# Weight product of a two-layer graph network on one core: seven products over pairs of row blocks, summed in PSUM

## The chip, the core and the metric

The kernel runs on one core of a Trainium2 chip. Time is device time in microseconds (us) of one execution. A core has five engines, each working through its own list of instructions in order: PE (matrix products; it writes only to PSUM), DVE (elementwise work, transposes, maxima), ACT (activation functions and copies), POOL and SP (here mostly issuers of DMA transfers). An instruction can wait for counts that instructions of other engines raise when they end. PSUM has eight banks; one bank holds 128 x 512 float32 numbers. SBUF is the large on-chip memory.

## The reference

Two layers over 4096 nodes with 512 features, and a 4096 x 4096 matrix of zeros and ones.

```
# layer 0: mean of the first 64 neighbours, two linear maps, residual, layer norm
keep = Ab & (cumsum(Ab, axis=1) <= 64);  nb_mean = keep @ X / max(cnt, 1)
x1 = layernorm(x + leaky(x @ W_line.T + b_line) + where(cnt > 0, leaky(nb_mean @ W_nb.T + b_nb), 0))
# layer 1: attention over the neighbours, residual, layer norm
Wh = x1 @ W + bW
e  = (Wh @ a1 + b1)[:, None] + (Wh @ a2 + b2)[None, :]
e  = where(adj > 0, leaky(e, 0.2), -9e15);  attention = softmax(e, axis=1)
out = layernorm(x1 + attention @ Wh)
```

Every row of `attention` sums to one, so `attention @ (x1 @ W + bW)` equals `attention @ (x1 @ W) + bW`. The scores come from a vector computed apart (`W @ a`), not from `Wh`.

## The kernel before

**Layer 0** (to 677 us of the profile) makes x1 in 32 blocks of 128 rows and stores them to DRAM in four tensors `x1_d[0..3]`.

**The weight product**, from 677 to 787 us, is the stage that changes. It makes Wh in 32 steps `s` (loop at L1060). A step takes a block of 128 rows of x1 (a "square" in the change's words: 128 rows, whose 512 features are the contraction), turned so that the features lie on the partitions, and multiplies it with the 512 x 512 weight: four matmuls 128x512 at L1064, accumulated in one PSUM bank (`acc`). Around them:

- `load_turned` (L799 to L807, the DMAs at L804) loads square s+7 by four DMAs on SP into one of four places `x1s`; `turn_x1` (L814, transpose at L818) turns square s+3 on DVE into a tile `c` (three of them, and three early places).
- `finish_wh` (L822, at L827) adds the bias `bias_w` on DVE and writes the step's result from PSUM into `bt`. `bt` has 16 entries of 7 parts of 128x256: an entry belongs to a pair of squares s and s+4, whose four half results are parts 0 to 3. `combine_wh` (L835, L840 to L843) makes the other operands of the seven products of the attention stage from them, four subtractions on DVE.
- From s = 7 the attention weights of the first two row blocks (b = 0 and 1, four quarters i each) are made beside the products: `cover` (ACT, L863), `mask` (DVE, L873, with a maximum beside it), `score` (ACT, L856), after four quarters `greatest` (eight small DVE instructions, L886 to L893), `bend_greatest` (four small ACT instructions, L856), `less` (DVE, L910) and `weigh` (ACT exponential, L919). One quarter is masked at each step s = 8 to 15.
- At s = 22 to 28 `turn` and `combine` (L938, L951 to L954) make the operands of the first two parts of the attention product, q = 0 and 1.

**The attention stage**, from 787 us to the end, is `consume(q)` for 64 parts q (PE, L978): 28 products of matmuls 128x256 each, seven for eight over pairs of row blocks. Beside it DVE and ACT make the weights of the next blocks; the four `combine_wh` left over run in q = 0. `load_res` (L991) loads the two rows of x1 of the residual by SP, some 48 us before `end_row` (L1022) adds them; then come the layer norm and the store on POOL.

The order of each engine's work is that of the Python text: the kernel schedules by hand (`manual_schedule`), and the recording layer adds a wait wherever two engines touch the same tile; for PSUM it does so by bank.

Of the kernel before, what the change touches and what calls it, by code (L numbers as in the profile page):

```python
# [9 lines left out]
F32 = mybir.dt.float32  # L10
# [5 lines left out]
ALU = mybir.AluOpType  # L16
# [4 lines left out]
P = 128  # L21
SQ = 32
# [10 lines left out]
def two_layer_adj_gnn(  # L33
# [16 lines left out]
    nc = tc.nc  # L50
    N, C = x.shape
    NB = N // P
    NC = C // P
    NT = NB // 2
# [46 lines left out]
    def x1_blk(b):  # L101

        n, k = divmod(b // 2, 4)
        return x1_d[k].rearrange("(n q r) c -> n r q c", n=4, r=2)[n, b % 2]
# [32 lines left out]
    with ExitStack() as l0:  # L137
# [130 lines left out]
        NS = NB // KB  # L268
# [516 lines left out]
    for n in range(NC):  # L785
        nc.sync.dma_start(
            ws[ts(n, SQ), :, :], w[ts(n, P), :].rearrange("(m b) c -> b m c", b=SQ)
        )
    bias_w = ep.tile([P, C], F32, name="res", bufs=1)


    bt = big.tile([P, NS // 2, 7, HC], F32, name="bt")
# [3 lines left out]

    st_n = big.tile([P, NI, 3, NB], F32, name="st_n")

    def load_turned(s):  # L799

        if s < NS:
            part = x1_d[s // 8].rearrange("(n s a) c -> s a n c", s=8, a=SQ)[s % 8]
            for n in range(NC):
                nc.sync.dma_start(  # L804
                    x1s[ts(n, SQ), s % 4, :].rearrange("a (j c) -> a j c", c=P),
                    part[:, :, ts(n, P)],
                )  # L807

# [2 lines left out]

    FIRST = 8

    def turn_x1(s):  # L814
        if s < NS:
            t = early[:, s, :C] if s < 3 else rows.tile([P, C], F32, name="c")
            x1ts[s] = t.rearrange("p (m i) -> p m i", i=P)
            nc.vector.transpose(  # L818
                x1ts[s].rearrange("p m (j a) -> p j m a", a=SQ),
                x1s[:, s % 4, :].rearrange("p (j m b) -> p j m b", m=NC, b=SQ),  # L820
            )

    def finish_wh(s):

        kk, h = s // 8 * 4 + s % 4, s // 4 % 2
        b = bt[:, kk]
        nc.vector.tensor_tensor(  # L827
            b[:, 2 * h : 2 * h + 2, :], pws.pop(s).rearrange("p (h c) -> p h c", h=2),
            bias_w.rearrange("p (h c) -> p h c", h=2), ALU.add,
        )  # L830
        if h == 1:
            later.append(kk)

    later = []

    def combine_wh():

        if later:
            b = bt[:, later.pop(0)]
            nc.vector.tensor_tensor(b[:, 4], b[:, 1], b[:, 0], ALU.subtract)  # L840
            nc.vector.tensor_tensor(b[:, 5], b[:, 3], b[:, 4], ALU.subtract)
            nc.vector.tensor_tensor(b[:, 6], b[:, 5], b[:, 2], ALU.subtract)
            nc.vector.tensor_tensor(b[:, 1], b[:, 3], b[:, 1], ALU.subtract)  # L843

    def load_nat(b, h):

        if b < NB:
            nats[b, h] = ep.tile([P, 2, NS * SQ // 2], BF16, name="nat")
            rows = code_d[b].rearrange("(i a) (n x) -> n a i x", a=SQ, n=4)
            for n in range(4):  # L850
                nc.sync.dma_start(nats[b, h][ts(n, SQ)], rows[n][:, ts(h, 2), :])
# [6 lines left out]
    def cover(b, i):  # L858

        if i == 0:  # L860
            wts[b] = early if b == 0 else wp.tile([P, NI, NS * SQ], F32, name="w")
            m4s[b] = stat.tile([P, NI], F32, name="m4", bufs=2)
        nc.scalar.activation(  # L863
            wts[b][:, i, :], nats[b, i // 2].bitcast(U8)[:, i % 2, :],
            AF.Relu, bias=far, scale=-FAR,
        )
        if i % 2:
            load_nat(b + 1, i // 2)

    def mask(b, i):  # L870

        w_i = wts[b][:, i, :]
        nc.vector.tensor_tensor_reduce(  # L873
            w_i, e2_n, w_i, 1.0, -3e38, ALU.subtract, ALU.max, m4s[b][:, i : i + 1]
        )

    def score(b, i):
        w_i = wts[b][:, i, :]
        bend1(b, i, w_i, w_i)

    def greatest(b):
        m4 = m4s.pop(b)
        mm = stat.tile([P, NI], F32, name="mm", bufs=2)
        m2 = stat.tile([P, NI], F32, name="m2", bufs=2)
        q0, q1, q2, q3 = (slice(SQ * n, SQ * n + SQ) for n in range(4))
        nc.vector.tensor_copy(m2[q0], m4[q1])  # L886
        nc.vector.tensor_copy(m2[q2], m4[q3])
        nc.vector.tensor_tensor(m4[q0], m4[q0], m2[q0], ALU.max)
        nc.vector.tensor_tensor(m4[q2], m4[q2], m2[q2], ALU.max)
        nc.vector.tensor_copy(m2[q0], m4[q2])  # L890
        nc.vector.tensor_tensor(mm[q0], m4[q0], m2[q0], ALU.max)
        for q in (q1, q2, q3):
            nc.vector.tensor_copy(mm[q], mm[q0])  # L893
        mms[b] = mm
# [7 lines left out]
    def bend_greatest(b):  # L902
        mm = mms.pop(b)
        lms[b] = stat.tile([P, NI], F32, name="lm", bufs=2)
        for i in range(NI):
            bend1(b, i, lms[b][:, i : i + 1], mm[:, i : i + 1])

    def less(b):
        nms[b] = stat.tile([P, NI], F32, name="nm", bufs=2)
        nc.vector.scalar_tensor_tensor(  # L910
            nms[b], lms.pop(b), -1.0, st_n[:, :, 1, b], ALU.mult, ALU.subtract
        )

    def weigh(b, i):
        g, r = divmod(b, 2)
        if i == r == 0:
            z4s[g] = stat.tile([P, 2, NI], F32, name="z4", bufs=2)
        w_i = wts[b][:, i, :]
        nc.scalar.activation(  # L919
            w_i, w_i, AF.Exp, bias=nms[b][:, i : i + 1], accum_out=z4s[g][:, r, i : i + 1]  # L920
        )
        if i == NI - 1:
            del nms[b]
            if r == 1:
                nc.sync.dma_start(z_d[g], z4s.pop(g))
                zqs[g] = stat.tile([P, 2, 4], F32, name="zq", bufs=2)
                for i_ in range(NI):
                    nc.sync.dma_start(
                        zqs[g][ts(i_, SQ)],
                        z_d[g].rearrange("(n a) r i -> i a r n", a=SQ)[i_],  # L930
                    )
# [52 lines left out]
    def load_res(g):  # L984

        for b in (2 * g, 2 * g + 1):
            if b % 2:
                x1rows[b] = ep.tile([P, C], F32, name="res", bufs=1)
            else:
                x1rows[b] = rows.tile([P, C], F32, name="c")  # L990
            nc.sync.dma_start(x1rows[b], x1_blk(b))  # L991

    def end_weights(g):
        rz = stat.tile([P, 2], F32, name="rz", bufs=2)
# [37 lines left out]
    for s in range(3):  # L1032
        turn_x1(s)
        load_turned(s + 4)
    nc.sync.dma_start(bias_w, b_w.partition_broadcast(P))
    for g in range(5):
        if g == 2:
            bend0(NB - 1)
# [18 lines left out]
    for n in range(4):  # L1057
        nc.gpsimd.dma_start(st_n[ts(n, SQ)], st_d.rearrange("(i a) k b -> a i k b", a=SQ))

    for s in range(NS):  # L1060
        pws[s] = ps_acc.tile([P, C], F32, name="acc")
        x1t = x1ts.pop(s)
        for m in range(NC):
            nc.tensor.matmul(  # L1064
                pws[s], x1t[:, m, :], ws[:, m, :], start=(m == 0), stop=(m == NC - 1)
            )
        if s > 0:
            finish_wh(s - 1)
        turn_x1(s + 3)
        load_turned(s + 7)  # L1070
        if s == 0:
            load_nat(0, 0)
            load_nat(0, 1)
        k = s - FIRST
        if k in (4, 8):
            less(k // NI - 1)
        if 0 <= k < 8:
            mask(*divmod(k, NI))
        if -1 <= k < 7:
            cover(*divmod(k + 1, NI))  # L1080
        if 0 <= k < 8:
            score(*divmod(k, NI))
        if k in (3, 7):
            greatest(k // NI)
            bend_greatest(k // NI)
        if 4 <= k < 12:
            weigh(*divmod(k - 4, NI))
        if s in range(FIRST + 14, FIRST + 22, 2):
            q, part = divmod((s - FIRST - 14) // 2, 2)
            (turn, combine)[part](q)  # L1090
        elif s >= FIRST + 8:
            combine_wh()
    finish_wh(NS - 1)

    for q in range(NP * NT):
        g, k = divmod(q, NP)
        consume(q)
        more = 0 < q < NP * NT - 1
        if more:
            turn(q + 1)  # L1100

        b = {2: 2 * g + 3, 3: 2 * g + 4}.get(k, 2 if q == 0 else NB)
        if k == 3 and more:
            combine(q + 1)
        if b < NB:
            for i in range(NI):
                cover(b, i)
                mask(b, i)
            for i in range(NI):
                score(b, i)  # L1110
            greatest(b)
        if k != 3 and more:
            combine(q + 1)
        if b < NB:
            shift(b)
            for i in range(NI):
                weigh(b, i)
        while q == 0 and later:
            combine_wh()
        if k == 0 and g > 0:  # L1120
            end_weights(g - 1)
            end_low(g - 1)
            end_top(g - 1)
        if q == NP * NT - 1:
            end_weights(g)
        if k == 1:
            if g > 0:
                end_row(2 * g - 2, nc.gpsimd)
                end_row(2 * g - 1, nc.gpsimd)
            load_res(g)  # L1130
# [65 lines left out]
```

## Time and profile before

| | us |
|---|---|
| three runs | 1568.65, 1570.67, 1571.28 (median 1570.67) |
| the profiled execution's own time | 1568.37 |
| its span (first to last instruction) | 1566.6 |
| PE, DVE, ACT, POOL busy | 1557.8, 1258.2, 952.7, 238.4 |
| the weight product, 677.05 to 786.92: length | 109.87 |
| in it PE, DVE, ACT, POOL busy | 109.87, 83.43, 32.96, 7.05 |
| attention stage, 786.92 to 859.00: PE, DVE, ACT busy | 72.08 of 72.08, 60.06, 45.38 |

A row of a group reads: line, engine, operation, what it writes and reads, shapes, count, then busy time and mean ns of one, then the engine's idle time before it and what ended that. A timeline row reads: start, length, engine, line, operation, count, and in brackets the idle time before it. A float32 matmul stands as two records, of weight load (PEld) and product (PE) each. Records of PE overlap: a 128x512 record is 0.59 long, and the next begins 0.43 after it began; a 128x256 record is 0.38 long and the next begins 0.216 later.

### The profile page before, as it was taken

To read this page: it belongs to the slowest core of one execution; us is meant where nothing else is said; L and a number is where in the kernel's file an instruction comes from. 1 tells how busy PE (TensorE), PEld (TensorE's weight loads), DVE (VectorE), ACT (ScalarE), POOL (GpSimd) and SP (SyncE) were. 2 spreads that over 40 slices of the span, in tenths; PEclk is the share of its full clock that TensorE was granted. 3 is DMA by queue.
4 is the path that set the end of the run, shared out by engine and by line. 5 is a ranking of instruction groups with operands and counts; after the bars stand their busy time and mean duration, and the time that the engine had idled before them with its cause. 6 is when DMAs were issued, how large, how long until landed. Compare 5 with 4: busy or idle time off the path is not lost.

```text
span 1566.6 us, 18624 instructions
## 1 busy us (share of the span) xinstructions
PE 1557.8 (99%) x6419; PEld 1211.5 (77%) x6419; DVE 1258.2 (80%) x2309; ACT 952.7 (61%) x1123; POOL 238.4 (15%) x393
## 2 busy tenths in 40 slices
PE   9999999999999999999999999999999999999998
PEld 5444468888888888854488888888888888888887
DVE  6888658989999898357888888788878878888765
ACT  2766558887888887417065675555765557655530
POOL 4554212222222122120000000000000000000000
PEclk9999999999999999999999999999999999999999
DMA  8865468889888987753111111110111111111101
GB/s 235 210 221 193 155 197 251 251 242 264 245 263 220 269 250 196 154 123 106 48 41 44 27 52 55 41 52 24 48 55 41 54 35 34 55 41 54 42 1 41
DMA packets 170878, 193.01 MB, mean 123 GB/s; under 512 B 101424, under 2 KB 134992, under 8 KB 162592
## 3 DMA queue, kind: packets, MB, share of 16 engines
q1 hardware_dynamic: 148256, 131.12, 29.5%
q0 software_dynamic: 21664, 59.27, 13.4%
q10 hardware_dynamic: 864, 1.44, 0.3%
q8 instruction: 50, 0.82, 0.2%
q14 instruction: 44, 0.36, 0.1%
HBM read 132.91 MB, written 42.08 MB: 112 GB/s over the span
## 4 chain that ended last, share of the span: by engine, by line
PE 98%; DVE 1%; issue 0%; ACT 0%; DMA 0%; POOLq 0%; DVEq 0%; ACTq 0%
PE acc L978 35%; PE acc L750 30%; PE pt L978 14%; PE acc L498 8%; PE acc L1064 7%; PE acc L372 3%; PE pt L372 0%; PE pt L153 0%; DVE edge L389 0%; DMA xb<-in_x_dram 0%; DVE left L194 0%; ACT edge L175 0%; DVE y_lo L421 0%; DVE xt L325 0%; ACT L175 0%
## 5 line engine op out<-in xcount | busy, mean ns | idle before, releaser
L978 PE MATMUL acc<-bt,s 128*128 128x256 f32 x1504 | 335.7, 379 | 0.0
L750 PE MATMUL acc<-y_hi,kt 128*128 128x512 f32 x824 | 320.5, 389 | 0.0
L750 PE MATMUL acc<-y_lo,kt 128*128 128x512 f32 x824 | 320.5, 389 | 0.0
L978 PEld LDWEIGHTS acc<-bt,s 128*128 128x128 f32 x1504 | 285.8, 190 | 38.9
L863 ACT ACTIVATE w<-nat,few 128x1024 f32<-128x1024 uint8 x128 | 136.8, 1135 | 293.0 <-DVE a L938 238.5
L978 PE MATMUL acc<-bt,a 128*128 128x256 f32 x1056 | 239.0, 379 | 0.0
L978 PE MATMUL pt<-bt,a 128*128 128x256 f32 x992 | 224.6, 379 | 0.0
L978 PEld LDWEIGHTS acc<-bt,a 128*128 128x128 f32 x1056 | 200.6, 190 | 27.3
L978 PEld LDWEIGHTS pt<-bt,a 128*128 128x128 f32 x992 | 188.5, 190 | 26.1 <-issue 0.5
L938 DVE STREAM_TRANSPOSE a<-w 128x1024 f32<-128x1024 f32 x128 | 153.0, 1225 | 62.0 <-ACT w L919 53.2
L277 ACT ACTIVATE kt<-ktb,few 128x1024 fp32r<-128x1024 uint8 x124 | 142.8, 1151 | 97.7 <-PE acc L750 80.5
L126 POOL TENSOR_TENSOR rs<-ve,few 128x1 f32<-128x1 f32 x64 | 46.5, 726 | 940.6 <-DVE ve L124 927.3
L750 PEld LDWEIGHTS acc<-y_hi,kt 128*128 128x128 f32 x824 | 154.7, 188 | 32.2
L750 PEld LDWEIGHTS acc<-y_lo,kt 128*128 128x128 f32 x824 | 154.6, 188 | 32.1
L856 ACT ACTIVATE w<-w,st_n 128x1024 f32<-128x1024 f32 x128 | 149.3, 1232 | 33.7 <-DVE m L873 33.7
L919 ACT ACTIVATE w<-w,nm 128x1024 f32<-128x1024 f32 x128 | 145.4, 1137 | 11.1 <-DVE nm L910 11.1
L873 DVE CUSTOM_DVE_ANT_0 w<-e_n,w 128x1024 f32<-128x1024 f32 x128 | 149.3, 1219 | 1.8 <-ACT w L863 0.5
L175 ACT ACTIVATE edge<-a,few 128x2048 bf16<-128x2048 int32 x64 | 136.2, 2128 | 6.0 <-issue 2.7
L223 ACT CAST code<-left 128x2048 uint8<-128x2048 bf16 x64 | 121.1, 1892 | 0.0
L1064 PE MATMUL acc<-w,c 128*128 128x512 f32 x232 | 99.7, 592 | 0.0
L1064 PEld LDWEIGHTS acc<-w,c 128*128 128x128 f32 x232 | 44.1, 190 | 55.5 <-issue 53.8
L206 DVE TENSOR_TENSOR left<-edge,left 128x2048 bf16<-128x2048 bf16 x64 | 78.4, 1225 | 2.2
(190 smaller groups left out, 1900.3 us busy)
## 6 DMA issues: line engine op xcount, KB each, us to landing
a<-in_adj_dram SPq DMA_DIRECT2D x64, 1024.0 KB, 6.1
code_d<-code POOLq DMA_DIRECT2D x64, 256.0 KB, 4.0
nat<-code_d SPq DMA_DIRECT2D x256, 64.0 KB, 2.0
w<-x_d SPq DMA_DIRECT2D x128, 64.0 KB, 2.0
own<-in_x_dram SPq DMA_DIRECT2D x31, 256.0 KB, 3.3
own<-own_d POOLq DMA_DIRECT2D x31, 256.0 KB, 4.8
x_d<-own POOLq DMA_DIRECT2D x31, 256.0 KB, 4.9
c<-in_x_dram POOLq DMA_DIRECT2D x120, 64.0 KB, 4.8
```

The source lines that it names most:

```text
L175: nc.scalar.activation(edge_of[s], loaded.pop(s).rearrange("p (t q) -> p q t", q=2), AF.Sigmoid, bias=steep[:, 0:1], scale=STEEP, accum_ou ...
L223: nc.scalar.copy(code.bitcast(U8).rearrange("p (t q) -> p q t", q=2), seen_of.pop(s))
L277: nc.scalar.activation(kts[s], bytes_.rearrange("p t (i r) -> p t r i", r=2), AF.Sigmoid, bias=steep[:, 1:2], scale=STEEP,)
L498: nc.tensor.matmul(bank, lhs[:, k, :], rhs[:, k, :], start=start and k == 0, stop=k == 1, skip_group_check=True,)
L750: nc.tensor.matmul(accs[i], kt[:, k // 2, k % 2, :], term[j], start=(j == 0 and term is y_hi), stop=(j == NB - 1 and term is y_lo),)
L856: nc.scalar.activation(dst, src, AF.Prelu, bias=bias, scale=scale, alpha=0.2)
L863: nc.scalar.activation(wts[b][:, i, :], nats[b, i // 2].bitcast(U8)[:, i % 2, :], AF.Relu, bias=far, scale=-FAR,)
L873: nc.vector.tensor_tensor_reduce(w_i, e2_n, w_i, 1.0, -3e38, ALU.subtract, ALU.max, m4s[b][:, i : i + 1])
L919: nc.scalar.activation(w_i, w_i, AF.Exp, bias=nms[b][:, i : i + 1], accum_out=z4s[g][:, r, i : i + 1])
L938: nc.vector.transpose(a[:, r].rearrange("p s (i a) -> p i s a", a=SQ), wts[2 * g + r][:, :, ts(k, 8 * SQ)].rearrange("p i (s x) -> p i s x ...
L978: nc.tensor.matmul(banks[g][n], lhs[:, j, :], bt[:, 4 * k + j, rhs, :], start=(k == 0 and j == 0 and n == mate[0]), stop=(k == NP - 1 and ...
L1064: nc.tensor.matmul(pws[s], x1t[:, m, :], ws[:, m, :], start=(m == 0), stop=(m == NC - 1))
```

## The change

The 32 squares of x1 are taken in another order, so that the squares of one entry of `bt` follow each other (`SEQ`; step j = 2g + h takes pair g, its upper square for h = 0 and its lower for h = 1). The first two pairs (`PLAIN = 2`) are multiplied as before. For the other 14 pairs the pair is a 2 x 2 block matrix (two squares, two halves of the contraction), the weight is another (two halves of the contraction, two halves of the columns), and seven products of blocks replace eight. A product is two matmuls 128x256 (`product_wh`). The products that several results share are not added on DVE but grow in PSUM: a pair has two banks, `yr` and `xv`, each of two halves. With m1 the first product:

- `yr[0]`: m1 (x11 by w11), copied out by ACT (L905), then x12 by w21 is added to it in the next pair's step;
- `yr[1]`: the second product, (x11 - x21) by `t3`; DVE adds m1 to it and writes `xv[0]` (L915; L911 for the first such pair); then s4 by w22 is added;
- `xv[0]`: that sum, to which s2 by `t2` is added; ACT copies it to `xv[1]` (L932); then x22 by `t4` is added to `xv[0]` and s1 by `t1` to `xv[1]`.

Each pair's products stand over two pairs' steps: PE's order in the steps of pair g is m1(g), second(g), x12 by w21 (g-1), s1 by t1 (g-1), x22 by t4 (g-1), s2 by t2 (g), s4 by w22 (g). ACT copies both finished banks into `bt` (L918, L928), where DVE added the bias before. DVE makes the sums of the weight once (`sums_w`, L864 to L866, and one in place at L1195, after the fourth plain square) and the sums of x1 for every pair (L876, L877, L882, L883). `combine_wh` has three instructions for these pairs. The bias is no longer in `bt`: for each of the 32 row blocks a DMA on POOL adds `b_w` to the residual row in SBUF (L1081). The attention weights of the first two blocks are spread out: a quarter is masked in every second step, j = 8 to 22, as `weights_step` says, and only the operands of part q = 0 are made in the stage; those of q = 1 are made in q = 0. Two of the left over `combine_wh` run in each of q = 1 and 2.

```diff
-    bias_w = ep.tile([P, C], F32, name="res", bufs=1)
+    SEQ = [8 * t + u + 4 * h for t in range(4) for u in range(4) for h in range(2)]
...
-    def finish_wh(s):
-        kk, h = s // 8 * 4 + s % 4, s // 4 % 2
-        b = bt[:, kk]
-        nc.vector.tensor_tensor(
-            b[:, 2 * h : 2 * h + 2, :], pws.pop(s).rearrange("p (h c) -> p h c", h=2),
-            bias_w.rearrange("p (h c) -> p h c", h=2), ALU.add,
-        )
...
     def combine_wh():
         if later:
-            b = bt[:, later.pop(0)]
-            nc.vector.tensor_tensor(b[:, 4], b[:, 1], b[:, 0], ALU.subtract)
-            nc.vector.tensor_tensor(b[:, 5], b[:, 3], b[:, 4], ALU.subtract)
+            kk = later.pop(0)
+            b = bt[:, kk]
+            if kk < PLAIN:
+                nc.vector.tensor_tensor(b[:, 1], b[:, 3], b[:, 1], ALU.subtract)
+            nc.vector.tensor_tensor(b[:, 5], b[:, 0], b[:, 1], ALU.add)
+            nc.vector.tensor_tensor(b[:, 4], b[:, 3], b[:, 5], ALU.subtract)
             nc.vector.tensor_tensor(b[:, 6], b[:, 5], b[:, 2], ALU.subtract)
-            nc.vector.tensor_tensor(b[:, 1], b[:, 3], b[:, 1], ALU.subtract)
...
+    def seven_wh(g, part, extra=lambda: None):
+        p = g - 1
+        new, old = g < NS // 2, p >= PLAIN
+        yr, xv = yrs[g % 2], xvs[g % 2]
+        yr_p, xv_p = yrs[p % 2], xvs[p % 2]
+        t1, t2, t3, t4 = wsums
+        m1 = bt[:, g, 2] if new else None
+        if part == 0:
+            if new:
+                product_wh(yr[:, 0], x1ts[2 * g][:, 0:2], w11, start=True)
+                nc.scalar.copy(m1, yr[:, 0])
+                product_wh(yr[:, 1], x1ts[2 * g + 1][:, 0:2], t3)
+            if old:
+                product_wh(yr_p[:, 0], x1ts.pop(2 * p)[:, 2:4], w21)
+                product_wh(xv_p[:, 1], sum_x(p, 1), t1)
+            if g == PLAIN:
+                nc.vector.tensor_tensor(xv[:, 0], m1, yr[:, 1], ALU.add)
+            turn_x1(2 * g + 3)
+            sums_x1(g + 1)
+            if new and g > PLAIN:
+                nc.vector.tensor_tensor(xv[:, 0], m1, yr[:, 1], ALU.add)
+            extra()
+            if old:
+                nc.scalar.copy(bt[:, p, 0:2], yr_p)
+        else:
+            if old:
+                product_wh(xv_p[:, 0], x1ts.pop(2 * p + 1)[:, 2:4], t4)
+            if new:
+                product_wh(xv[:, 0], sum_x(g, 2), t2)
+                product_wh(yr[:, 1], sum_x(g, 4), w22)
+            turn_x1(2 * g + 4)
+            sums_x2(g + 1)
+            if old:
+                nc.scalar.copy(bt[:, p, 2:4], xv_p)
+                later.append(p)
+            extra()
+            if new:
+                nc.scalar.copy(xv[:, 1], xv[:, 0])
...
             nc.sync.dma_start(x1rows[b], x1_blk(b))
+            nc.gpsimd.dma_start(x1rows[b], b_w.partition_broadcast(P), accum_op=ALU.add)
...
+    def weights_step(j):
+        k = j - FIRST
+        i, rest = divmod(k, 2)
+        if k in (8, 16):
+            less(k // 8 - 1)
+        if rest == 0 and 0 <= i < 8:
+            mask(*divmod(i, NI))
+        if rest == 1 and -1 <= i < 7:
+            cover(*divmod(i + 1, NI))
+        if rest == 1 and 0 <= i < 8:
+            score(*divmod(i, NI))
+        if k in (6, 14):
+            greatest(k // 8)
+            bend_greatest(k // 8)
+        if k in (10, 12, 14, 16):
+            weigh(0, (k - 10) // 2)
+        if 17 <= k < 20:
+            weigh(1, k - 17)
+        if k == 19:
+            weigh(1, 3)
+        if k == 20:
+            turn(0)
+        if k == 22:
+            combine(0)
+        if j in (8, 9) or k in (5, 9, 13, 15, 16, 17, 18, 19):
+            combine_wh()
...
+    for j in range(NS):
+        g, h = divmod(j, 2)
+        if g < PLAIN:
+            ...
+        else:
+            seven_wh(g, h, lambda: weights_step(j))
+        load_turned(j + 7)
+        if j in (3, 5):
+            load_nat(0, j // 4)
+        if j in (5, 7):
+            combine_wh()
+    seven_wh(NS // 2, 0)
+    seven_wh(NS // 2, 1)
...
-        more = 0 < q < NP * NT - 1
+        more = q < NP * NT - 1
```

## The prediction

> **What bounds the kernel now.** I read the chain of waits first, then the busy time of the stage, then single rows for prices. In the chain around the stage PE's work stands unbroken, with no other engine in it:
>
> ```profile
> 639.81 37.40 PE acc L750 x165
> 677.21 109.87 PE acc L1064 x256
> 787.08 3.45 PE pt L978 x16
> ```
>
> So the stage's length is PE's 128 matmuls 128x512 at 109.87 / 128 = 0.858 each, or 6.87 for the eight of a pair of squares. The busy time of the stage and of the one after it:
>
> ```profile
> 677.05:786.92 109.87, 109.87 (x258) 48.64 (x257) 83.43 (x171) 32.96 (x44) 7.05 (x12) 1.00 0.37 93
> 786.92:859.00 72.08, 72.08 (x335) 63.46 (x334) 60.06 (x123) 45.38 (x63) 2.31 (x4) 1.00 0.15 45
> ```
>
> PE is busy for all of it (second and third column), at a granted clock of 1.00; DVE 83.43, ACT 32.96. PE's work counts one for one, and so does each wait that PE is given. Before, PE has none here: what it reads was turned three squares earlier, and six banks take turns. The change gives it one per pair, so its prices matter most:
>
> ```profile
> 787.12 0.69 DVE L827 TENSOR_TENSOR bt<-acc,res 128x512 f32<-128x512 f32 x1 [0.40 <-PE acc L1064]
> 786.92 1.46 PE L978 MATMUL pt<-bt,a 128*128 128x256 f32 x6
> L1006 ACT COPY c<-pt 128x256 f32<-128x256 f32 x15 | 5.3, 351 | 2.5 <-PE pt L978 2.5
> 47.17 0.69 DVE L582 TENSOR_TENSOR acc<-lo,acc 128x512 f32<-128x512 f32 x1
> 47.92 1.98 PE L498 MATMUL acc<-wt_line,lo 128*128 128x512 f32 x4 [0.59 <-DVE acc L582]
> 42.02 1.88 PE L498 MATMUL acc<-hi,xt 128*128 128x512 f32 x4
> ```
>
> A reader of PSUM starts 0.20 after PE could have gone on (787.12 against 786.92). A copy of 128x256 out of PSUM lasts 0.35. PE goes on 0.06 after the writer it waited for (47.86 to 47.92), and its first matmul then costs 0.10 more (four take 1.98 for 1.88), as its weight load isn't ahead.
>
> **Products: 11.6 less.** 14 pairs x 8 matmuls 128x512 = 112 x 0.858 = 96.1 go. 14 x 7 products of two matmuls 128x256 come; a part of the attention stage, 28 such matmuls, takes 12.08 in the chain (3.45 + 8.63), so a product costs 0.863, and 98 cost 84.6. The four plain squares keep 13.7. Without a wait the stage would last 98.3: 11.6 less.
>
> **The wait in every pair: 14 x 0.71 = 9.9.** m1 goes to `yr[0]`, ACT copies it out (L905), and the second product goes to `yr[1]`, in the same bank. In the built program the first matmul of the second product waits for the count that this very copy raises, in all 14 pairs. PE works in order, so the finished operands behind it wait too. With ACT free: 0.20 to the copy, 0.35, 0.06, 0.10 = 0.71. The nearest rows bound a free round trip at 0.5 and 0.9. [...]
>
> **ACT is late in the dense pairs: 7 x 0.4 = 2.8.** In the steps of pairs 4 to 10 ACT has, in this order after x22 by t4: the 128x512 copy of the old pair (0.59, the next begins 0.50 after its start), cover (two in 2.19: 1.05), score (1.14 to the next), the copy `xv[0]` to `xv[1]` (0.30), then the next m1's copy (0.35). That is 0.20 + 0.50 + 1.05 + 1.14 + 0.30 + 0.35 + 0.16 = 3.70 until PE goes on, where its three products last 2.59: a wait of 1.1 instead of 0.71, in pairs 5 to 11. Pair 14 comes behind two exponentials (2 x 1.13 for cover and score): 0.5 more.
>
> **The maximum holds a bank: 2.3 and 2.1 + 0.7.** ACT's order bites once more for each of the two row blocks. The four small ACT instructions on the maximum stand ahead of the copy of the old pair's `yr`, and the next m1 needs that bank.
>
> ```profile
> 720.32 0.16 DVE L886 COPY m<-m 32x4 f32<-32x4 f32 x1
> 721.44 0.51 DVE L893 COPY mm<-mm 32x4 f32<-32x4 f32 x3
> 736.02 1.21 ACT L856 ACTIVATE lm<-mm,st_n 128x1 f32<-128x1 f32 x4
> 737.14 1.13 ACT L919 ACTIVATE w<-w,nm 128x1024 f32<-128x1024 f32 x1
> ```
>
> Pair 7, from its start: second product ends at 0.86 + 1.10 + 0.86 = 2.82, DVE's sum begins 3.02 and its mask 3.40, ends 4.55, the eight small ones (720.20 to 721.95) 6.30, the four of ACT 7.45, the copy 8.04; m1 of pair 8 at 8.2 instead of 7.14: 1.05. ACT is then behind: second copy, cover, score, two copies end in a go for the second product at 11.4, where PE was ready at 9.06: 2.35, 1.25 above the 1.1. In pair 11 an exponential (1.13) stands there too: m1 of pair 12 at 9.3 for 7.14, 2.15; then 0.65 above 0.71, as no cover is left.
>
> **The first seven-product pair: 1.0.** The in-place sum of the weight waits for the last plain square (0.19), takes 0.69; then come two sums of x1 (0.45, 0.42): the second product may start 1.75 after m1 did, for 0.86 + 0.71; 0.25. There alone nothing stands between the second product and s2 by t2, which needs DVE's sum: 0.20 + 0.42 + 0.16 = 0.78.
>
> **Sum.** 98.3 + 9.9 + 2.8 + 0.5 + 2.3 + 2.8 + 1.0 = 117.6, against 109.87: **7.7 longer**. The profiled execution's own 1568.37 becomes 1576.1. The three runs' median lies 2.3 above it, so I say **1578.4** for a median.
>
> **What I cost at nothing, and its cover.** DVE in a dense pair: two transposes (0.64 start to start), four sums (1.7), the sum to PSUM (0.4), a mask (1.15), three of `combine_wh` (1.25): 5.8 of 7.1, idle for the rest; without PE's waits a pair is 6.04, and it would be full. Bias addition (32 x 0.68 on DVE) goes to ACT copies, which I priced where they stand in the way. Loads of x1: SP issued 32 in 18.60 about 692, 0.58 each; a pair has 8 and at most 4 others (7.0 at that pace, 5.2 at the median of 0.43), with four squares of lead. The mask's vectors landed by 702 (last issue 697.2, 4.5 to land); the first mask comes near 706. At the end of the stage the operands of q = 1 (two transposes 2.3, four sums 2.7) move behind it: `a` and `s` come free with PE's last three products, so they are done some 3.5 after the stage's end, 8.5 before q = 1. The later masks stand behind them, but q = 2 starts 24 later and DVE was busy 16.3 of 20 there; that margin takes it up. The 32 bias DMAs: 0.92 issue and 4.8 landing of the accumulating DMA before, 48 ahead of use; POOL waits for SP's load there, and only norms due 48 later are queued behind. Cover gone, one would cost some 5, at the end alone, where it has 36. SP loses one load of the bias.
>
> **Rivals.**
> 1. Not slower: PE's wait is cheap. It decides at the round trip: the ground terms leave 11.6 to spend, and first pair, dense pairs and maximum spend 9.4, so with them it would have to be under 0.16. If ACT's late order were absorbed (all but the first pair's 1.0) and a free round trip took 0.5, the stage would last 106.3: 1567 in a median. For: that copy is short. Against: each of its four parts has a row. With 0.71 and all else absorbed: 109.2, no change.
> 2. Slower still: ACT or DVE fall behind their rows. ACT's order is a chain; 0.15 more per PSUM copy, of which two stand in the chain, and DVE full in pairs 8 to 14 would add some 0.5 in each of 14 pairs: 7, 1585. For: DVE's and ACT's lists are in one order with PE's. Against: 1.3 of slack per pair on DVE.
> 3. The clock falls in PE's waits. The row: at 47 to 50 PE had a gap of 0.59 (its weight load idled 1.42) and the granted clock stayed 1.00; my longest waits are 2.4. [...] Half speed over one pair's 7.1 behind each of the two longest would cost 3.5 each: 1585.
> 4. The change doesn't do what it says, as products of 256 columns cost more than half of 512. The attention stage's row denies it (0.863 for two).
>
> **How the numbers follow.** Within 0.2% is within 3.1 of 1570.7, about what a measurement here can tell. Forecast with its sizes off by up to 4: 0.62, slower. Rival 1: 0.22, of it 0.10 faster and 0.12 same. Rival 2: 0.11; rival 3: 0.05, both slower. The range from 1568.0 (free waits) to 1586.0 (rival 2) leaves out under 2 in 10. Faster 0.10, same 0.12, slower 0.78.
>
> **What would show it.** PE idle in the stage near 19, most of it before L887 and put down to ACT L905; two gaps of over 2, after the maxima; span between the first L1184 and the first product of the attention stage near 117.6. Wrong, if PE's products follow m1 without a gap, if DVE's transposes end PE's waits, or if gaps stand behind the stage.

## The result, and the profile after

| | us |
|---|---|
| changed kernel, four runs | 1578.16, 1584.02, 1584.03, 1585.94 (median 1584.03) |
| kernel before, four runs | median 1569.94 (1568.65 to 1571.28) |
| ratio | 1.0083, 95% interval 1.0055 to 1.0111 |
| the profiled execution after: own time, span | 1585.94, 1584.2 |

Slower, by 14.1 us, and inside the range; the forecast was 1578.4, so some 6 of the 14 weren't foreseen. Busy time of the stage and of all that follows it, after the change (columns: stretch, its length, then PE, PEld, DVE, ACT, POOL, the granted clock, DMA share, GB/s):

```profile
680.25:804.38 124.13, 107.75 (x426) 82.10 (x424) 86.66 (x200) 58.68 (x103) 7.06 (x12) 0.96 0.34 80
804.38:1584.20 779.82, 773.71 (x3585) 680.77 (x3583) 621.66 (x1238) 443.44 (x617) 66.00 (x94) 1.00 0.22 53
```

The stage lasts 124.13 where it lasted 109.87: 14.26 more. What follows lasts 779.82 (before: 1566.6 - 786.92 = 779.68), so the loss is in the stage alone. This execution also began the stage 3.2 later (680.25 for 677.05), by waits in its first 80 us; in the second profile of the same kernel, shown below, the stage began at 677.11, so that part belongs to the execution. The mean granted clock of the stage is 0.96: it was 1.00 before. PE's waits in the stage:

```profile
PE acc L887 <- ACT bt L905: 12.7, 14, 2.1
PE acc L887 <- ACT bt L918: 2.7, 2, 1.9
PE acc L887 <- DVE acc L911: 0.6, 1, 0.6
PE acc L887 <- DVE acc L915: 0.3, 1, 0.3
```

Fourteen waits for the copy of m1 (L905), two for the copy that stands behind the maximum (L918), one in the first pair (L911). That is the forecast's list, but for the 0.3 behind L915 in pair 3. Now PE's timeline around the first long wait, in pairs 7 and 8:

```profile
728.77 1.03 PE L887 MATMUL acc<-w,a 128*128 128x256 f32 x4
730.69 1.13 PE L887 MATMUL acc<-w,a 128*128 128x256 f32 x4 [0.89 <-ACT bt L905]
...
735.11 1.03 PE L887 MATMUL acc<-w,bt 128*128 128x256 f32 x4
736.94 1.13 PE L887 MATMUL acc<-w,a 128*128 128x256 f32 x4 [0.80 <-ACT bt L918]
740.17 1.47 PE L887 MATMUL acc<-w,c 128*128 128x256 f32 x4 [2.10 <-ACT bt L905]
741.44 1.91 PE L887 MATMUL acc<-w,a 128*128 128x256 f32 x4
743.15 1.57 PE L887 MATMUL acc<-s,bt 128*128 128x256 f32 x4
```

A group of four records is one product. Ends of records are modelled and overlap what comes next by 0.17 (a product is 1.03 long, and the next begins 0.86 after it), so a bracket of 0.89 is a gap of 1.06. Read the second column: 1.03 is the usual length (1.13 behind a wait), but the three products behind the 2.10 last 1.47, 1.91 and 1.57. What ACT did meanwhile:

```profile
735.20 1.22 ACT L945 ACTIVATE lm<-mm,st_n 128x1 f32<-128x1 f32 x4 [4.56 <-DVE mm L982]
736.33 0.56 ACT L918 COPY bt<-acc 128x512 f32<-128x512 f32 x1
736.79 0.58 ACT L928 COPY bt<-acc 128x512 f32<-128x512 f32 x1
737.27 1.15 ACT L952 ACTIVATE w<-nat,few 128x1024 f32<-128x1024 uint8 x1
738.32 1.23 ACT L945 ACTIVATE w<-w,st_n 128x1024 f32<-128x1024 f32 x1
739.45 0.37 ACT L932 COPY acc<-acc 128x256 f32<-128x256 f32 x1
739.75 0.37 ACT L905 COPY bt<-acc 128x256 f32<-128x256 f32 x1
```

ACT stood 4.56 for DVE's maximum (L982), and all that was queued behind it came in a go; m1's copy is the last. And the clock, in slices of 1 us:

```profile
740.00:741.00 1.00, 0.82 (x3) 0.70 (x4) 0.00 (x0) 0.12 (x1) 0.00 (x0) 0.92 0.37 107
741.00:742.00 1.00, 1.00 (x4) 0.81 (x3) 0.24 (x1) 0.00 (x0) 0.00 (x0) 0.50 0.00 0
...
744.00:745.00 1.00, 1.00 (x6) 0.90 (x5) 0.96 (x4) 0.00 (x0) 0.00 (x0) 0.88 0.00 0
```

The granted clock (third column from the end) is 0.50 from about 740.8 to 744.2: 3.4 us. Behind pair 12's wait of 1.94 it is 0.50 from 771.6 to 778.4: 6.8 us. What that cost is read against the same products at full clock. From the second product of pair 8 to that of pair 9 it takes 8.89 here (740.17 to 749.06) and 7.20 in the second profile, where no fall followed; from the second product of pair 12 to that of pair 13 it takes 9.39 here and 6.77 in the kernel with the waits filled (both below). So 1.7 + 2.6 = 4.3 us were lost (m1 of pair 12 was slow as well, but the wait for ACT behind it ended no later for that). That is most of the 6.5 by which the stage is longer than the forecast's 117.6.

### The profile page after: what moved, and what is told of

Read it like the earlier page. It is cut to its first block, busy times and chain, and to the rows that moved or that the text cites. A ratio compares the mean times of both kernels' runs of the same rounds, so it can differ in the third digit from the quotient of the medians.

```text
span 1584.2 us, 19149 instructions
## 1 busy us (share of the span) xinstructions
PE 1557.2 (98%) x6587; PEld 1246.1 (79%) x6587; DVE 1262.6 (80%) x2337; ACT 979.0 (62%) x1183; POOL 269.4 (17%) x425
## 4 chain that ended last, share of the span: by engine, by line
PE 91%; DMA 3%; ACT 2%; DVE 2%; issue 1%; SPq 0%; POOL 0%; POOLq 0%; DVEq 0%; ACTq 0%
PE acc L1067 35%; PE acc L750 29%; PE pt L1067 14%; PE acc L498 7%; PE acc L887 3%; PE acc L372 2%; DMA a<-in_adj_dram 1%; DMA c<-in_x_dram 1%; ACT w L945 1%; DMA w<-x_d 1%; PE pt L372 0%; DMA a<-in_L_gnn_W_nb_dram 0%; POOL c L298 0%; DMA nat<-code_d 0%; SPq L807 0%
## 5 line engine op out<-in xcount | busy, mean ns | idle before, releaser
L298 POOL DMA_DIRECT2D c<-in_x_dram x120 | 66.0, 558 | 71.0 <-DVE xt L325 57.4
L194 DVE TENSOR_TENSOR_SCAN left<-few,ends,left 128x1024 bf16<-128x1024 f32 x32 | 75.2, 2352 | 1.1
```

## The experiments

Each edit is made to the changed kernel. Times are medians; the kernel before, run beside them on the same chips, had 1567.7 to 1568.0.

| kernel | time | ratio to before, 95% | stage | PE waits |
|---|---|---|---|---|
| the change, once more | 1580.83 | 1.0085 (1.0072 to 1.0098) | 120.51 | 14.6 |
| long waits filled | 1576.60 | 1.0054 (1.0042 to 1.0066) | 118.52 | 10.1 |
| only the shorter of them filled | 1578.38 | 1.0064 (1.0051 to 1.0076) | 120.87 | 13.2 |
| mask loads early | 1583.68 | 1.0104 (1.0085 to 1.0123) | 130.53 | 18.8 |
| maximum two squares later | 1571.37 | 1.0021 (1.0013 to 1.0030) | 112.87 | 10.5 |
| second product one later | 1568.44 | 1.0003 (0.9994 to 1.0012) | 109.35 | 7.0 |
| second product two later | 1569.66 | 1.0010 (1.0001 to 1.0019) | 110.68 | 8.6 |
| bias DMAs left out | 1577.53 | 1.0064 (1.0050 to 1.0078) | 120.43 | 14.4 |
| maximum later, second one later | 1562.24 | 0.9964 (0.9952 to 0.9977) | 104.07 | 1.8 |
| maximum later, second two later | 1561.14 | 0.9958 (0.9944 to 0.9971) | 103.23 | 2.9 |

(Stage and waits are those of each kernel's profiled execution, the waits as the sum of the view's lines. The first two kernels, the mask loads and the maximum were run on one chip; the second products, the shorter waits and the bias on another; the last two on a third.)

### The change once more

> The changed kernel as it is, once more beside the others. My theory of its 14.1 us: the waits of TensorE for the copies of m1 (about 14 us in the stage with their restarts), two long waits near its middle behind ScalarE's wait for VectorE's maximum (pairs 8 and 12, 3.1 and 2.8 us), and behind each of these two a stretch at half clock that the forecast had put at nothing (4.4 to 4.8 us in the profiled execution: four-matmul groups of 1.4 to 2.1 us where 1.03 is usual). If so, a profile of it shows the same two long waits again (1.9 to 2.3 us each) and slow groups right behind them, and its times lie between 1578 and 1586. Rival, that the slow groups came by chance in one execution: no slow groups here, a stage of about 119.5 instead of 124.1, and times near 1578.

1580.83 (1579.18 to 1582.67), stage 120.51. Both long waits are there again, at the same 2.10 and 1.94, but only the second is followed by slow groups (768.24: 1.91; half clock for 6.8 us); behind the 2.10 the products last 1.13 and 1.03. So the waits are fixed by the order of the instructions, and whether the clock falls behind them differs from one execution to the next (the last section sets the two profiles side by side). The five runs show it too: the mean granted clock of an execution was 0.997 at 1579.18 and 0.995 at 1582.67. Pair 4's wait, 1.74 in the first profile, is 0.46 here.

### The long waits filled with matmuls of no use

```diff
+    def spin(n):
+        idle_b = ps_s.tile([P, 2, HC], F32, name="pt")
+        for k in range(n):
+            nc.tensor.matmul(
+                idle_b[:, 0], bt[:, 0, 0, :P], bt[:, 0, 1], start=True, stop=True,
+                skip_group_check=True,
+            )
...
             if new:
+                if g in (8, 12):
+                    spin(2 if g == 8 else 4)
                 product_wh(yr[:, 0], x1ts[2 * g][:, 0:2], w11, start=True)
                 nc.scalar.copy(m1, yr[:, 0])
+                if g in (8, 12):
+                    spin(5 if g == 8 else 2)
                 product_wh(yr[:, 1], x1ts[2 * g + 1][:, 0:2], t3)
```

> In pairs 8 and 12 TensorE is given matmuls of no use while it would wait (2 ahead of m1 and 5 ahead of the second product in pair 8, 4 and 2 in pair 12, each 128x256 and by the profile 0.43 us, into a bank that nothing reads). Nothing of the result changes. Clock theory: the products start when they did, the granted clock stays at 1.00 in the whole stage, and 4.4 to 4.8 us go: stage 119.5, time about 1579.5, ratio to before 1.006. Rival, that the slow groups behind the waits have another cause (weight loads, a port, the copies beside them): the groups stay at 1.4 to 2.1 us, the stage at 124, or a few tenths more by what the matmuls of no use overhang the waits; time 1584.

1576.60: 4.2 less than the change beside it, as the clock theory said (1579.5 had been reckoned from the first profile's time). PE's timeline in pair 8 (L895 is the matmul of no use):

```profile
731.00 1.03 PE L895 MATMUL pt<-bt 128*128 128x256 f32 x4
731.97 1.13 PE L887 MATMUL acc<-w,a 128*128 128x256 f32 x4
732.94 2.32 PE L895 MATMUL pt<-bt 128*128 128x256 f32 x10
735.20 1.13 PE L887 MATMUL acc<-w,c 128*128 128x256 f32 x4
736.17 1.03 PE L887 MATMUL acc<-w,a 128*128 128x256 f32 x4
```

From m1 to the second product it takes 3.23 as it did with the waits empty (736.94 to 740.17), since ACT is as late as before; but the products behind it last 1.13 and 1.03, and every slice of the stage has a clock of 1.00. Nothing was taken from the computation and nothing moved on ACT or DVE: doing useless work made the kernel 4 us faster. That settles the clock, 0.50 without these matmuls and 1.00 with them, as the cause of the slow groups.

### Only the shorter waits filled

```diff
+                if g == 8:
+                    spin(2)
                 product_wh(yr[:, 0], x1ts[2 * g][:, 0:2], w11, start=True)
                 nc.scalar.copy(m1, yr[:, 0])
+                if g == 12:
+                    spin(2)
                 product_wh(yr[:, 1], x1ts[2 * g + 1][:, 0:2], t3)
```

> Matmuls of no use fill only the shorter wait of the two in pair 8 (2 of them ahead of m1, 0.8 us) and in pair 12 (2 ahead of the second product, 0.6 to 0.8); the longer ones, 2.10 and 1.94 us, stay empty. This asks what lets the clock fall: if one empty stretch of about 2 us is enough, the slow groups are there as in the change (in pair 12 at least, since there they began with m1, ahead of the shorter wait) and the time is 1579 to 1581; if it takes both waits close together, they are gone and the time is that with all waits filled, 1576.6.

1578.38, between the two ends. In the profile half clock follows both empty stretches, the 2.10 of pair 8 and the 1.94 of pair 12, for 3.4 us each. So here one empty stretch, of 2.10 or 1.94 us, was enough. In pair 12 it is 3.4 here and 6.8 in both profiles of the change, where another wait (0.76 and 0.61) followed; but with the bias DMAs left out a second wait of 0.46 went with 3.4. The last section sets these cases beside PE's busy time.

### The maximum's bend later

```diff
         if k in (8, 16):
+            bend_greatest(k // 8 - 1)
+        if k in (9, 17):
             less(k // 8 - 1)
...
         if k in (6, 14):
             greatest(k // 8)
-            bend_greatest(k // 8)
```

> ScalarE's four small operations on the maximum are issued two squares later (at the 8th and 16th square counted from square 8 and not the 6th and 14th), and VectorE's subtraction one square later, so that ScalarE no longer stands waiting 4.56 us for VectorE's maximum with copies behind it that TensorE needs. My theory: the wait of 0.8 and 1.94 us at m1 of pairs 8 and 12 goes, the one of 2.10 at the second product of pair 8 falls to about 0.9, and with them the two stretches at half clock: 0.97 + 1.3 + 2.1 + 4.5 = 8.9 us less; time about 1575, ratio 1.003. If the clock has nothing to do with the waits, 4.4 us less: 1579.6. Rival, that VectorE is late as such and the wait comes back at the subtraction or at the weights behind it: less than 3 us.

1571.37, 9.5 less than the change (8.9 had been expected). The waits of the stage are now:

```profile
PE acc L887 <- ACT bt L905: 9.9, 14, 1.0
PE acc L887 <- DVE acc L911: 0.6, 1, 0.6
```

No wait for L918 is left, none is over 1.0, and the clock is 1.00 throughout. Two waits on ACT for DVE's maximum had cost 5 us directly and some 4 more through the clock (4.2 by the kernel with the waits filled). The rival (VectorE late as such) falls.

### The second product one and two places later

One later:

```diff
                 nc.scalar.copy(m1, yr[:, 0])
-                product_wh(yr[:, 1], x1ts[2 * g + 1][:, 0:2], t3)
             if old:
                 product_wh(yr_p[:, 0], x1ts.pop(2 * p)[:, 2:4], w21)
+            if new:
+                product_wh(yr[:, 1], x1ts[2 * g + 1][:, 0:2], t3)
+            if old:
                 product_wh(xv_p[:, 1], sum_x(p, 1), t1)
```

> TensorE's order in a pair is changed alone: m1, then the earlier pair's x12 times w21, then the second product into m1's bank, then s1 times t1; with the change the second product stood right behind m1. So 0.86 us of other matmuls lie beside ScalarE's copy of m1. Theory (the wait is for that copy alone, because both products are in one bank): the gap of 0.63 in the pairs 3, 4, 13 and 15 closes, the dense pairs (5 to 7, 9 to 11) and 14 keep 0.2 to 0.3 of theirs, pair 8 keeps 1.4 and pair 12 next to none; 2.5 + 5.2 + 0.9 + 0.9 + 0.9 = 10.3 us less, and the long waits at m1 of pairs 8 and 12 (0.8 and 1.9) stay, with a stretch at half clock behind the second. Stage 109 to 110, time 1570 to 1571 (1580.8 for the change itself, measured last). Rival (ScalarE or VectorE is late as such, and the wait only shows at that product): the waits move to m1 or to s2 times t2, and less than 4 us goes.

1568.44, 12.4 less than the change (12.1 if each is taken against the kernel before beside it: 0.7 and 12.8 longer); the stage is 109.35, where it was 109.87 before. The waits:

```profile
PE acc L887 <- ACT bt L920: 4.5, 2, 2.8
PE acc L887 <- ACT bt L905: 1.9, 3, 1.2
PE acc L887 <- DVE acc L913: 0.6, 1, 0.6
```

Of the 14 bracketed waits for m1's copy three are left (pair 2, which has no older pair's work; pair 8's 1.24; one of 0.2). In the dense pairs a rest of about 0.2 stays that is too short for a bracket: there the second product still lasts 1.13 and starts 1.00 to 1.06 after the one ahead of it, where 0.86 is usual. The waits didn't move to s2 by t2, so ACT and DVE aren't late as such. What had been expected to stay, the waits at m1 of pairs 8 and 12, grew instead: 1.67 and 2.81 for 0.80 and 1.94, by the 0.87 that PE came earlier, because the maximum's time is DVE's. In this profile the clock stayed at 1.00 behind the 2.81.

Two later:

```diff
                 nc.scalar.copy(m1, yr[:, 0])
-                product_wh(yr[:, 1], x1ts[2 * g + 1][:, 0:2], t3)
             if old:
                 product_wh(yr_p[:, 0], x1ts.pop(2 * p)[:, 2:4], w21)
                 product_wh(xv_p[:, 1], sum_x(p, 1), t1)
+            if new:
+                product_wh(yr[:, 1], x1ts[2 * g + 1][:, 0:2], t3)
```

> The same, with the second product one place later again, behind s1 times t1: 1.73 us beside the copy of m1, but only 0.86 us between the second product and s2 times t2, which needs VectorE's addition behind it (pair 2, which has nothing between, waits 0.59 there). Wait theory: the rest of 0.2 to 0.3 in the dense pairs and 0.86 in pair 8 go as well, 2.4 us more than with the step above; the cover of VectorE's addition shrinks to 0.86, and where VectorE is busy with a turn of x1 (about 1 us) up to 0.5 us comes back in some pairs. Together 1 us under the kernel above: stage 108 to 109, time 1569 to 1570. Rival: the addition is late in every pair and 13 x 0.5 = 6.5 us come back: 1575 to 1577.

1569.66: the time was in the expected span, but for other reasons; it is 1.2 above the kernel it was to beat by 1. The waits at m1 became 2.53 and 3.67, and behind the 3.67 the clock was at half for 3.4 us. The cover gained over the copy was paid back at the maximum, and some 1.5 more by the clock (an estimate: half of the 3.06 us of products that ran at half clock).

### The mask's loads early

```diff
-        if j in (3, 5):
-            load_nat(0, j // 4)
+        if j == 0:
+            load_nat(0, 0)
+            load_nat(0, 1)
```

> Both loads of the packed mask for block 0 are issued at square 0, as in the kernel before, and not at squares 3 and 5. My theory: pair 4's wait of 1.74 us at the second product goes to the 0.5 to 0.6 of the pairs beside it, since cover no longer waits for the transfer (ScalarE had waited 2.51 us for it): -1.2 us; and 0.3 to 0.6 more if the turned loads of x1 come earlier, too. Time about 1582.5. Rival, that the queue was behind for the turned loads' own sake: pair 4 shows a wait of VectorE for x1 in its place and the time is as with the change, 1584, or up to 1 us more because the loads of the mask now stand ahead of x1's.

1583.68, over 1578.68 to 1589.50: 2.9 above the change beside it. Pair 4's wait is at 0.46, but pair 3 has a new one. First DVE's row, then PE's:

```profile
700.23 0.71 DVE L833 STREAM_TRANSPOSE a<-w 128x512 f32<-128x512 f32 x1 [4.41 <-DMA w<-x_d]
```

```profile
705.23 2.07 PE L887 MATMUL acc<-s,bt 128*128 128x256 f32 x4 [3.84 <-DVE acc L915]
707.10 1.91 PE L887 MATMUL acc<-w,bt 128*128 128x256 f32 x4
```

And SP's queue, where L807 loads x1:

```profile
SPq L807 <- DMA nat<-code_d: 2.9, 1, 2.9
```

The eight mask loads ahead on the queue held up a square of x1: DVE waited 4.41 for it, PE 3.84 behind DVE, and the clock fell there too (half for 6.8 us). In this execution the rival's direction holds, and its price was too small. But the profiled execution is the slowest of the six, and the fastest, 1578.68, is under the fastest of the change beside it (1579.18); the two intervals of the ratio overlap. So the loss isn't there in every execution, and that the late place of the loads is the cheaper one isn't shown.

### The bias DMAs left out

```diff
-            nc.gpsimd.dma_start(x1rows[b], b_w.partition_broadcast(P), accum_op=ALU.add)
```

> Left out: the 32 DMAs on POOL's queue that add b_w to the residual's rows (the output lacks b_w). My reading, that they are hidden: the stage and what follows it (779.8 us in the profiled execution) keep their lengths, time 1580.8 within 1.5. Rival, that they cost something by traffic or through POOL's queue: some 1 to 3 us less behind the stage.

What follows the stage lasts 1576.7 - 796.95 = 779.75 us, against 779.82 with them and 779.68 before: the DMAs are hidden. The stage (120.43) equals that of the change's second profile (120.51). The median is 3.3 under the change's 1580.83, more than the 1.5 allowed; the runs' mean clocks (0.996 to 0.998, for 0.995 to 0.997) suggest fewer slow stretches, but no profile shows why there should be fewer, and the two kernels were not run beside each other. That difference stays open, and comparisons here between kernels run on different chips are to be read with these 3 us in mind.

### Both edits together

These hold the edit of the maximum's bend and one of the two edits of the second product, as shown above:

> Two edits together: the second product one place later (behind x12 times w21), and ScalarE's operations on the maximum two squares later. Theory: what they save adds up, since they close different waits. The first alone left a stage of 109.35 with 4.5 at m1 and 1.24 at the second product of pair 8, all of them behind the wait for the maximum; without those and their restarts the stage is 103, with no stretch at half clock; time 1562, ratio 0.996. Rival: with TensorE faster, ScalarE and VectorE are the next to be late (both are busy 5 to 8 of 10 us in the stage) and the gain is under 3 us: 1566 or more.

> The same with the second product behind s1 times t1. Alone that left 110.68, of which 6.2 at m1 of pairs 8 and 12, 0.94 behind pair 8, and a stretch at half clock of about 1.7 us come from the wait for the maximum: stage 101.5, time 1560.5, ratio 0.9955. Rival as above; where VectorE's addition is late in dense pairs, 1 to 2 us more than the kernel above.

1562.24 with a stage of 104.07, and 1561.14 with 103.23: the savings add up, and ACT and DVE don't take the place of the waits. Both beat the kernel before, by 5.6 and 6.7 us. The stage of the second, and PE's waits in it:

```profile
675.76:778.99 103.23, 100.25 (x425) 78.77 (x424) 86.31 (x200) 58.49 (x103) 7.04 (x12) 1.00 0.39 97
```

```profile
PE acc L887 <- DVE acc L916: 1.4, 2, 1.0
PE acc L887 <- DVE acc L912: 0.6, 1, 0.6
PE acc L887 <- ACT bt L905: 0.5, 1, 0.5
PE acc L887 <- ACT acc L933: 0.4, 1, 0.4
```

DVE's addition (L916) now ends two waits, as had been feared, but at 1.4 in all. With 98.3 for the products alone (the forecast's figure) there are 5 us left in the stage.

## Why the prediction was right in sign and 6 us short

- **Products, 11.6 less.** Right: products follow each other by 0.86 in the rows above, and with the waits nearly gone the stage comes down to 103.23, of which 2.98 is idle.
- **The wait in every pair, 0.71.** Right: the gap is 0.46 + 0.17 = 0.63, and the first product behind it lasts 0.10 longer: 0.73. That the cause is m1's copy, and not a late ACT, is shown by the kernel with the second product one place later.
- **Dense pairs, 1.1; pair 14, 1.21.** Right: 0.84 to 0.89 in brackets, so 1.11 to 1.16; pair 14 0.98, so 1.25.
- **The maximum holds a bank.** Right in mechanism and size: m1 of pair 8 at 1.07 for 1.05, its second product at 2.37 for 2.35, m1 of pair 12 at 2.21 for 2.15. Pair 12's second product was given 1.36; it had 0.7 to 1.0 where m1 ahead of it was itself slowed by the clock, and 1.33 in the profile where m1 ran at full clock (mask loads early).
- **The first pair, 1.0.** About right: 0.86 for 0.78 at s2 by t2, but the 0.25 for the sum of the weight did not show.
- **Costed at nothing: DVE, bias DMAs, the operands of q = 1.** Right: what follows the stage keeps its length to 0.2.
- **Costed at nothing: the loads on SP.** Wrong by a little, and not in every execution. In the first profile ACT's cover waited for the mask's load, so that pair 4 waited 1.74 (0.46 in the second), and s2 by t2 of pair 3 waited 0.3: together 1.9 more than in the second profile. "Four squares of lead" were too thin a cover.

```profile
707.37 1.15 ACT L952 ACTIVATE w<-nat,few 128x1024 f32<-128x1024 uint8 x1 [2.51 <-DMA nat<-code_d]
```

- **Rivals 1 and 2.** A cheap wait (rival 1) is excluded by 0.73 a pair. ACT and DVE slower than their rows (rival 2) is, too: the dense pairs' waits lie within 0.06 of the 1.1 given, and once the order was changed, DVE's 86.3 and ACT's 58.5 of busy time fitted into a stage of 103.
- **The clock: the step that failed.** The forecast kept the stage at full speed and gave rival 3 five in a hundred. Its row showed a gap of 0.59 without a fall; that the clock would also hold through waits of 2.4, four times as long, is a term that no run shows, and the runs showed 0.50 behind nine of the twelve waits of 1.94 to 2.81. The price was bounded from one side only. The bound from the other side stood in the text (3.5 for each of the two waits, 7 in all) and measured 4.3 in the first profile, 2.5 in the second and 4.2 between the medians with and without the waits filled. The measured 1584.0 lay inside the range because its upper end had been set for rival 2; what took the time there was another cause, so that much was luck.

The sum shows it. With the long waits filled, the clock at 1.00 and the rest as changed, the stage lasts 118.52, of which 0.55 is pair 4's wait for a load: 118.0, where the forecast had 117.6. The measured waits, each with its 0.27 (0.17 hidden, 0.10 behind it), add up to the same: 98.3 for the products, 5 x 0.73, 1.11 + 5 x 1.16 for the dense pairs, 1.25 for pair 14, 1.07 + 2.37 and 2.21 + 1.33 behind the maxima and 0.86 in the first pair are 118.0; no term of the forecast is off by more than 0.4. In the first profile: 118.0 + 4.3 for the clock + 1.3 for pair 4 + 0.6 for pair 3 = 124.2, measured 124.13. In the second: 118.0 + 2.5 for the clock = 120.5, measured 120.51. So the forecast without rival 3 was right to half a microsecond, and rival 3 was not a rival but came on top.

## What to carry to other kernels

When products that share a bank are pulled apart by a copy of the first, put other products between them: here one place in PE's order was worth some 12 us, where the whole change had lost 12.8. Look for the wait of an engine that stands in the middle of a producer's queue (ACT for DVE's maximum): all that is queued behind it arrives late, and here two such waits were worth 9.5. And where TensorE is the bound, a wait may cost more than its own length: here nine of the twelve waits of 1.94 to 2.81 us had 3.4 or 6.8 us at a clock of 0.50 behind them, which is 1.7 us on top, or up to 3.4 (an estimate: half of the slow time), and matmuls of no use in the waits of pairs 8 and 12 took 4.2 us off the median.

## What the runs showed of the hardware that was not expected

The forecast kept the granted clock at 1.00. In the profiles it fell to 0.50 behind waits of 1.94 us and more, and not behind each of them. Over the profiles of these kernels (waits of PE in the weight product, as bracketed):

| wait of PE | how many | half clock behind it |
|---|---|---|
| up to 1.74 us | all the others | none |
| 1.94 to 2.81 us | 12 | 9 |
| 3.67 and 3.84 us | 2 | 2 |

Waits and falls don't map one to one: the same 2.10 was followed by a fall in four of five profiles; a 2.53 and the 2.81 weren't. One of the nine fell only after another 1.06 had followed the 1.94. The length of a slow stretch was 3.4 or 6.8 us in all eleven cases.

The places of the falls are not scattered. In the first profile the falls at 740.83 and 771.55 are 30.72 us apart, nine times 3.41, the length of its shorter slow stretch. With the mask loads early the slices of 10 us from 700 and from 770 have 0.69 and 0.77, which puts the falls at 703.8 and 775.4, 71.6 apart: twenty-one times that length. So the profiles that have a fall are cut here into steps of 3.41 us, counted from that fall; that the steps run on unchanged between falls is an estimate from these distances. Two such steps, from the first and the second profile of the change, show a difference (third column, PE's busy time). The first ends at the fall at 740.83 and holds the whole 2.10 of pair 8. The second ends nine steps ahead of that profile's fall at 764.7, in the middle of the same wait (733.07 to 735.17), and holds the 0.81 at m1 and the first 0.92 of the 2.10:

```profile
737.42:740.83 3.41, 1.31 (x7) 0.83 (x6) 0.76 (x2) 2.70 (x4) 0.00 (x0) 1.00 0.48 134
730.58:733.99 3.41, 1.69 (x7) 0.83 (x5) 2.53 (x6) 3.41 (x8) 0.00 (x0) 1.00 0.42 120
```

Behind the first the clock fell, behind the second it didn't. PE's busy time in such steps:

| step | PE busy, of 3.41 us | clock behind it |
|---|---|---|
| second product two later, the 3.67 | under 0.3 | half |
| the change, pair 8's 2.10 | 1.31 | half |
| the change, pair 12's 1.94, both profiles | 1.47 | half |
| the change, pair 4's 1.74 | 1.67 | full |
| the change once more, pair 8's 0.81 and 0.92 of its 2.10 | 1.69 | full |

All eleven falls follow a step with PE busy for 1.47 or less; no step of the weight product with 1.67 or more had one behind it. So here 1.94 us without products in a step of 3.41 was enough, and a 2.10 that the end of a step cut in two passed. The half clock lasted a second step where PE was busy for 2.80 or less of the first (five cases) and ended where it was busy for 2.95 or more (six). The profile with the second product one later has no fall in the stage from which to count, so its 2.81 without a fall is not placed.

What happens between 1.47 and 1.67 was not measured, and neither was what sets the steps.
